# A decoder layer on one core: a new order of instructions, other buffers, and identity products in TensorE's planned waits

## The chip, the cores and the metric

The kernel runs on one core of a Trainium2 chip. The metric is the device time of one execution in microseconds. A core has five engines with their own instruction queues: TensorE (PE in the profile; its weight loads are shown as PEld), VectorE (DVE), ScalarE (ACT), GpSimd (POOL) and SyncE (SP), which here issues all transfers.

## The reference

One layer of a decoder, in float32, on `x` of 4 batches x 512 tokens x 512 features. Cut to what matters:

```python
x = x + attention(layernorm(x))        # gated delta rule, 16 heads, DK = 96, DV = 192
x = x + routed(layernorm(x), ctx)      # 64 sets a batch, the best 2 of 4 allowed ones
x = x + ffn(layernorm(x))              # 512 -> 2048 -> 512, ternary weights, 8-bit inputs

# attention: q, k, v = silu(causal conv of 4 taps (h @ W)); q and k normalized to length 1
# beta = 2 sigmoid(h @ Wb); g = -exp(A_log) softplus(h @ Wa + dt_bias); for each token, each head:
S = S * exp(g_t)
S = S + outer(k_t, (v_t - k_t @ S) * beta_t)
o_t = q_t @ S
# out = (o * rsqrt(mean(o * o) + eps) * norm_weight * silu(h @ Wg)) @ Wo
```

## The kernel before, in words

The recurrence is worked in chunks of 128 tokens (`NC` = 4 a batch). Inside a chunk it becomes a triangular system for each head, whose inverse is formed once. The work goes in 16 steps, one for each batch and group of four heads:

- `batch_head` (once a batch, stage "head"): loads `x`, normalizes it, transposes it on TensorE into `hT`, and computes the decays `egt`, `egs`, `egc` and `beta`.
- `keys`: `project4` projects four heads' keys. `project` is the common part: a weight tile `w`, four products of 128x512 into a PSUM bank `mm`, one ScalarE operation and three VectorE operations for the taps into `acc`. Then come transposes into `kt`, the decay matrix `dec` and the triangular matrix `lm`.
- `invert` (stage "inv"): 31 pairs of VectorE operations solve the 32x32 diagonal blocks, then products of 32x32 and 64x64 on TensorE join them.
- `queries`, and twice a step `pair` (two heads each): `values` (stage "value") projects and transposes the values through VectorE and through DRAM (`turn`), stage "gate" projects the gates, stage "rec" runs over the four chunks, stage "out" normalizes, gates, transposes through DRAM and multiplies by `Wo`.
- `ternary` (in three of the steps): makes the ternary weights. The 16 tiles of 128 tokens of `feed_forward` then run `route` (the sets) and `ffn`: products of fp8 weights, Silu, quantization, transposes in bf16, and the output product.

TensorE writes to eight PSUM banks: three `mm`, two `tp`, three `ch`. The rest lives in one SBUF tile `mem`, cut by the kernel into named slots (`acc` 6, `w` 6, `s` 16 and so on), which is why the profile calls all of them `mem`.

What sets the order: nothing of this is issued while the functions run. A `Recorder` notes each operation with its engine, a cost in us (`cost`), what it depends on and which slots it takes. `order` then plays a list scheduler: at each moment the engine that can start first takes, among its ready operations, the one that starts earliest and, among equals, the one with the earliest due time `due`. Due times are worked backwards from the ends of the steps, `PERIOD` apart; the work for the next step (`keys`, `invert`) is moved by `LEAD` steps, and the table `SHIFT` moves each stage and each pair of stage and engine. A slot is taken when an operation starts and is free again when its last user is done. `emit` issues the operations in this order, so each engine's queue is fixed before the kernel runs, and on the chip each engine works its queue in order and waits only for what an operation reads or overwrites. All instructions are issued in one line of `emit`, so the profile shows line 529 for nearly all; groups are told apart by the names of the PSUM banks and by shapes.

The constant `cst` holds the identity (`C_ID`) and three triangular masks; it is the fifth transfer in SP's queue, after the first four tiles of `x`.

Of the kernel before, what the change touches and what calls it, by code (L numbers as in the profile page):

```python
# [10 lines left out]
F32 = mybir.dt.float32  # L11
# [30 lines left out]
PERIOD = 122.1  # L42
LEAD = 0.95
PERIOD2 = 6.0
TERNARY = 7
SETUP = 12
WORDS = 53200
SHIFT = {
    "ffn": 7.2,
    "ffn gpsimd": -501.1,  # L50
    "ffn scalar": 226.0,
    "ffn tensor": -105.9,
    "ffn vector": -438.8,
    "gate": 13.2,
    "gate scalar": 366.7,
    "gate tensor": 48.8,
    "head": -306.9,
    "head gpsimd": 120.3,
    "head scalar": 380.7,
    "head tensor": 370.6,  # L60
    "head vector": 365.7,
    "inv": 43.1,
    "inv gpsimd": 87.6,
    "inv scalar": -17.2,
    "inv tensor": -19.3,
    "inv vector": -220.0,
    "keys": 66.8,
    "keys gpsimd": 154.5,
    "keys scalar": 1187.1,
    "keys tensor": -173.2,  # L70
    "keys vector": -244.9,
    "out": 73.2,
    "out gpsimd": 147.6,
    "out scalar": 80.4,
    "out tensor": 100.6,
    "out vector": -377.3,
    "query": 23.1,
    "query gpsimd": 248.2,
    "query scalar": -308.3,
    "query tensor": -17.1,  # L80
    "query vector": -276.0,
    "rec": -96.3,
    "rec scalar": 101.1,
    "rec tensor": -613.6,
    "rec vector": -466.5,
    "route": 23.3,
    "route gpsimd": 151.3,
    "route scalar": -481.0,
    "route tensor": -177.3,
    "route vector": 424.0,  # L90
    "tern": 18.9,
    "tern scalar": 117.0,
    "tern tensor": -135.8,
    "tern vector": 483.9,
    "value": -315.1,
    "value scalar": 255.5,
    "value tensor": -1022.2,
    "value vector": -580.5,
    "wo": 201.9,
    "wo scalar": -256.6,  # L100
# [205 lines left out]
class Recorder:  # L306
# [67 lines left out]
    def cost(self, op, engine, method, args, kw, outs, ins):  # L374

        n = max(free_elems(x) for x in outs[:1] + ins)
        if engine == "tensor":
            if method == "transpose":
                n = free_elems(args[2])
                return 0.12 if kind(args[1]) == F32 else 0.07  # L380
            m = free_elems(args[1])
            n = free_elems(args[2])
            if kind(args[1]) == F32:
                return max(n / 600.0, m / 555.0) + 0.012
            return max(n / 2400.0, 0.06 * m / 128) + 0.004
        if engine == "vector":
            if method == "scalar_tensor_tensor":
                return n / 960.0 + 0.21
            if method == "tensor_tensor_scan":
                return n / 480.0 + 0.21  # L390
            if method == "tensor_scalar" or (method == "tensor_copy" and not in_psum(ins[0])):
                return n / 1920.0 + 0.22
            return n / 960.0 + 0.15
        if engine == "scalar":
            f = args[2].name if method == "activation" else ""
            f = next((s for k, s in ACT_SETS.items() if f.lower() == k.lower()), None)
            op.table = f or op.table
            extra = (0.19 if "accum_out" in kw else 0.0) + (0.07 if len(ins) > 1 else 0.0)
            return n / 1230.0 + 0.2 + extra
        if engine == "gpsimd":  # L400
            if ALU.pow in args:
                return 0.155 * n + 0.44
            if method in ("tensor_tensor", "tensor_mul", "tensor_add", "tensor_sub"):
                return max(0.2, n * 0.0022 + 0.05)
            return n * 0.0009 + 0.235
        op.nbytes += outs[0].nbytes() if not isinstance(outs[0], View) else outs[0].ap.nbytes()
        return 0.38
# [13 lines left out]
    def order(self, period, shift):  # L421
# [23 lines left out]
        while len(done) < len(ops):  # L445
            best = None
            for e, queue in engines.items():
                pick = None
                for o in queue:
                    t = max(o.ready, clock[e])  # L450
                    if pick is not None and t > pick[0]:
                        continue
                    need = self.room(o)
                    if need is None:
                        continue
                    t = max(t, need)
                    if e == "scalar" and o.table not in (None, table):

                        key = (t, o.due + 2.6)
                    else:  # L460
                        key = (t, o.due)
                    if pick is None or key < pick[:2]:
                        pick = key + (o,)
                if pick is not None and (best is None or pick[0] < best[0]):
                    best = (pick[0], e, pick[2])
# [56 lines left out]
    def emit(self, tc, period, shift):  # L522
        self.done = self.order(period, shift)
        real = lambda x: x.real() if isinstance(x, View) else x
        with tc.manual_schedule():
            for o in self.done:
                engine = getattr(self.nc, o.engine)
                for method, args, kw in o.calls:
                    getattr(engine, method)(  # L529
                        *[real(x) for x in args], **{k: real(v) for k, v in kw.items()}  # L530
                    )
# [26 lines left out]
def decoder_layer(ctx: ExitStack, tc: tile.TileContext, a: dict, out: bass.AP):  # L558
# [23 lines left out]
    w.rec.emit(tc, PERIOD, SHIFT)  # L582
# [51 lines left out]
def attention(w, a):  # L634
# [15 lines left out]
    xs, wos, gs, tw, gw, vs, os_ = w.xs, w.wos, w.gs, w.tw, w.gw, w.vs, w.os  # L650
# [18 lines left out]
    t_wg = slots("wg", 1, [P, KC * GV])  # L669
# [15 lines left out]
    t_oq = slots("oq", 1, [P, HG * DV])  # L685
    t_o2 = slots("o2", 1, [P, DV])
    t_oT = slots("oT", 2, [P, GV])
    t_sq = slots("sq", 1, [P, NC * DK])
    t_b = slots("b", 12, [P, NC * H])
    t_s = slots("s", 16, [P, 4 * NC], ordered=False)  # L690
# [13 lines left out]
    def turn(src, blocks, there):  # L704

        dve.transpose(blocks, src)
        for q in range(P // BS):
            sp.dma_start(
                there[q], blocks[q * BS : (q + 1) * BS].rearrange("i (t j) -> i t j", j=BS)
            )  # L710

    def batch_head(b):
# [4 lines left out]
        for i in range(NC):  # L717
# [12 lines left out]
            act.copy(hT[:, :, i * P : (i + 1) * P], pt)  # L730
        pba = p_tp(P, NC, 2 * H)
        for t in range(NC):
            for kc in range(KC):
                pe.matmul(
                    pba[:, t], hT[:, kc, t * P : (t + 1) * P], wba[:, kc],
                    start=kc == 0, stop=kc == KC - 1,
                )
        sh = [P, NC, H]
        beta = s["beta"] = t_b(*sh)
# [4 lines left out]
        z = t_b(*sh)  # L744
# [21 lines left out]
        pgt = p_tp(H, NC, P)  # L766
        with rec.group():
            for t in range(NC):
                pe.transpose(pgt[:, t], g[:, t], ident)
        gT = t_acc(H, T)  # L770
        act.copy(gT, pgt.rearrange("h t p -> h (t p)"))
        sp.dma_start(gs[b], gT)
# [3 lines left out]
        pg = p_tp(P, 3, NC * H)  # L776
        pe.matmul(pg[:, 0], le, gf, start=True, stop=True)
# [7 lines left out]
    def project(wsrc, hT, taps):  # L785

# [12 lines left out]
        return acc  # L799

    def project4(key, f, hT, taps, t_dst):
# [3 lines left out]
        for i in range(3):  # L805
            rec.hold(*dst)
            acc = project(a[key][f, i], hT, taps[:, i])
            act.activation(dst[i], acc[:DK], AF.Silu)
            act.activation(dst[3][32 * i : 32 * i + 32], acc[DK:P], AF.Silu)
        return dst  # L810

    def keys(s, f):
# [4 lines left out]
        k = s["k"] = project4("wk", f, s["hT"], cqk[:, 0, f], t_k)  # L817
        kt = s["kt"] = [t_kt(P, NC, DK) for _ in range(4)]
        ss = t_s(P, 4, NC)
        for j in range(4):  # L820
# [6 lines left out]
            sq = t_sq(P, NC, DK)  # L827
# [103 lines left out]
    def queries(s, f):  # L931

        rec.stage = "query"
        q = s["q"] = project4("wq", f, s["hT"], cqk[:, 1, f], t_q)
        ssq = s["ssq"] = t_s(P, 4, NC)
        for j in range(4):
            pk = p_tp(P, NC, DK)
            sq = t_sq(P, NC, DK)
            rec.hold(sq)
            with rec.group():  # L940
                for c in range(NC):
                    pe.transpose(pk[:, c], q[j][:, c * P : (c + 1) * P], ident[:DK, :DK])
            act.activation(sq, pk, AF.Square)
            dve.tensor_reduce(ssq[:, j], sq, AX.X, ALU.add)
        pool.tensor_scalar(ssq, ssq, EPS * DK, EPS * EPS * DK, ALU.mult, ALU.add)
        for j in range(4):
            pa = p_tp(P, NC, P)
            with rec.group():
# [5 lines left out]
    def values(s, hg, jo):  # L954
# [3 lines left out]
        for vt in range(NVT):  # L958
            rec.hold(*vo)
            acc = project(a["wv"][hg, vt], s["hT"], cv[:, hg * NVT + vt])  # L960
            act.activation(acc, acc, AF.Silu)
            there = vs[s["b"], hg, :, vt * P : (vt + 1) * P]
            turn(acc, t_acc(P, T), there.rearrange("(t i) (c j) -> c i t j", i=BS, j=BS))
# [8 lines left out]
    def pair(s, hg, jo, last):  # L972

        h0 = hg * HG
        k, q, lm, mq, kt = s["k"], s["q"], s["lm"], s["dec"], s["kt"]
        egt, egc = s["egt"], s["egc"]
        vo = values(s, hg, jo)
        rec.stage = "gate"
# [3 lines left out]
        for c in range(NC):  # L982
            g = t_gate(P, HG, DV)
# [7 lines left out]
            act.activation(g.rearrange("p j v -> p (j v)"), pp, AF.Silu)  # L991
            gate.append(g)
# [6 lines left out]
        for c in range(NC):  # L999
# [3 lines left out]
            if c:  # L1003
# [4 lines left out]
                for j in range(HG):  # L1008
                    dve.scalar_tensor_tensor(
                        rz[:, j], pr[:, j], egt[:, c, h0 + j : h0 + j + 1], vo[c][:, j],  # L1010
# [22 lines left out]
            if c:  # L1033
# [4 lines left out]
                for j in range(HG):  # L1038
                    act.activation(oq[:, j], pq[:, j], AF.Copy, scale=egt[:, c, h0 + j : h0 + j + 1])
# [433 lines left out]
```

## Time and profile before

| | |
|---|---|
| median of 3 runs | 2455.29 us (2452.61 to 2458.24) |
| the profiled execution | 2456.92 us |
| its span, first to last instruction | 2455.1 us |
| mean granted TensorE clock | 0.961 |
| busy: DVE, ACT, POOL | 1928.6, 1291.9, 856.3 us |
| DMA | 294.66 MB, mean 120 GB/s |

PE is one of five engines that wait for each other; its busy time says how much of the span it worked, and the granted clock at what rate. A page's slice is a fortieth of the span, 61 us. The span holds three parts: a start in which the first inputs, keys and inverse are made (to about 170 us), the 16 steps, and from about 2100 us on the feed-forward tiles, the first of which run among the last steps.

### The profile page before, as it was taken

Reading aid. Unit: us, or ns where it says so; the run is one execution under the profiler, and the core shown is the slowest. Engines: PE = TensorE matmul, PEld = TensorE weight load, DVE = VectorE, ACT = ScalarE, POOL = GpSimd, SP = SyncE. Lnnn points to the kernel's source line nnn. Section 1 sums busy time; section 2 is a strip of 40 time slices with the busy share of each in tenths; the row PEclk is TensorE's granted clock in tenths of the full one; section 3 lists DMA queues with packets and bytes.
Section 4 is the critical chain, followed back from the end, with each engine's and each line's share of the span. In section 5 each row is a group of like instructions: output and inputs, shape, how many; then the busy total and the mean of one; then the engine's idle time right before and its main releaser. Section 6 shows DMA issues by size and latency. Waiting matters only on the chain.

```text
span 2455.1 us, 36566 instructions
## 1 busy us (share of the span) xinstructions
PE 2314.4 (94%) x12230; PEld 1412.0 (58%) x12230; DVE 1928.6 (79%) x3594; ACT 1291.9 (53%) x2780; POOL 856.3 (35%) x1275
## 2 busy tenths in 40 slices
PE   8869999999999999999999999999999999999886
PEld 5455656575565656575656565665656565644432
DVE  5888888887858788887978899886979786677653
ACT  4555554555454666564563645345466454645442
POOL 4042413334032333343232332333333331566653
PEclk9969999999999999999998999999999999999888
DMA  5446443635463555656655645663535444422000
GB/s 188 134 130 161 104 111 82 147 77 137 108 164 72 149 146 146 164 137 164 169 155 131 154 113 140 161 158 86 148 94 138 96 137 105 112 63 66 22 13 17
DMA packets 579003, 294.66 MB, mean 120 GB/s; under 512 B 424000, under 2 KB 495936, under 8 KB 578560
## 3 DMA queue, kind: packets, MB, share of 16 engines
q1 hardware_dynamic: 578816, 292.34, 45.8%
q8 instruction: 97, 1.59, 0.3%
q14 instruction: 90, 0.74, 0.1%
HBM read 223.93 MB, written 68.29 MB: 119 GB/s over the span
## 4 chain that ended last, share of the span: by engine, by line
PE 68%; DVE 18%; ACT 6%; POOL 5%; issue 3%; DMA 1%; SPq 0%; POOLq 0%; DVEq 0%; ACTq 0%
PE mm L529 42%; DVE mem L529 18%; PE ch L529 16%; PE tp L529 10%; POOL mem L529 5%; ACT mem L529 5%; ACT L529 1%; DMA vs<-mem 0%; DMA mem<-vs 0%; SPq L529 0%; DMA mem<-in_wv 0%; DMA mem<-in_x 0%; DMA tw<-mem 0%; POOLq L1469 0%; DVEq L529 0%
## 5 line engine op out<-in xcount | busy, mean ns | idle before, releaser
L529 PE MATMUL mm<-mem 128*128 128x512 f32 (+3 forms) x3760 | 1556.4, 551 | 33.7 <-issue 13.7
L529 POOL TENSOR_TENSOR mem<-mem 128x2 f32<-128x2 f32 (+4 forms) x864 | 713.0, 839 | 768.7 <-ACT mem L529 483.5
L529 PEld LDWEIGHTS mm<-mem 128*128 128x128 f32 (+2 forms) x3504 | 637.6, 193 | 559.8 <-issue 422.0
L529 ACT ACTIVATE mem<-mem 128x192 f32<-128x192 f32 (+5 forms) x1361 | 673.3, 523 | 511.4 <-DVE mem L529 323.3
L529 DVE SCALAR_TENSOR_TENSOR mem<-mm,mem 128x511 f32<-128x511 f32 (+4 forms) x656 | 465.1, 730 | 177.1 <-ACT mem L529 152.4
L529 PE MATMUL ch<-mem 128*128 128x192 f32 (+3 forms) x2688 | 559.5, 347 | 16.3 <-ACT mem L529 9.4
L529 PE MATMUL tp<-mem 32*32 32x32 f32 (+6 forms) x5782 | 395.5, 230 | 86.4 <-DVE mem L529 50.6
L529 PEld LDWEIGHTS ch<-mem 128*128 128x128 f32 (+2 forms) x2176 | 363.7, 186 | 138.7 <-issue 42.0
L529 PEld LDWEIGHTS tp<-mem 32*32 32x32 f32 (+3 forms) x5462 | 336.0, 141 | 183.4 <-issue 79.2
L529 DVE TENSOR_REDUCE mem<-mem 128x4 f32<-128x384 f32 (+29 forms) x660 | 332.4, 507 | 59.7 <-POOL mem L529 31.4
L529 POOL TENSOR_SCALAR mem<-mem 128x1 f32<-128x1 f32 (+2 forms) x352 | 123.0, 350 | 582.7 <-ACT mem L529 370.7
L529 DVE STREAM_TRANSPOSE mem<-mem 128x512 f32<-128x512 f32 (+3 forms) x368 | 279.3, 762 | 43.8 <-POOL mem L529 25.1
L529 ACT ACTIVATE mem<-mm,mem 128x512 f32<-128x512 f32 x192 | 130.8, 683 | 248.5 <-PE mm L529 248.1
L529 DVE TENSOR_TENSOR mem<-mem 128x64 f32<-128x64 f32 (+28 forms) x553 | 248.4, 450 | 15.4 <-POOL mem L529 2.2
L529 ACT COPY mem<-tp 32x512 f32<-32x512 f32 (+6 forms) x292 | 172.3, 602 | 84.3 <-PE tp L529 81.8
L529 PEld LDWEIGHTS <-mem 128*128 128x128 bf16 x1088 | 98.4, 104 | 156.5 <-issue 35.8
L529 DVE SCALAR_TENSOR_TENSOR mem<-ch,mem 128x192 f32<-128x192 f32 (+1 forms) x272 | 127.9, 507 | 66.2 <-PE ch L529 63.2
L529 DVE TENSOR_TENSOR mem<-mem,mm 128x512 f32<-128x512 f32 x144 | 97.7, 682 | 54.4 <-PE mm L529 52.9
L529 ACT ACT_TABLE_LOAD x87 | 111.6, 1283 | 28.9 <-DVE mem L529 26.9
L529 DVE TENSOR_TENSOR mem<-tp,mem 128x512 f32<-128x512 f32 (+1 forms) x132 | 86.8, 668 | 46.3 <-PE tp L529 35.8
L529 ACT COPY mem<-ch 128x384 f32<-128x384 f32 x128 | 60.8, 475 | 87.4 <-PE ch L529 86.5
L529 ACT ACTIVATE mem<-ch,mem 128x192 f32<-128x192 f32 x192 | 70.5, 416 | 53.9 <-PE ch L529 53.6
(27 smaller groups left out, 568.6 us busy)
## 6 DMA issues: line engine op xcount, KB each, us to landing
mem<-in_wg SPq DMA_DIRECT2D x32, 768.0 KB, 4.7
mem<-in_wv SPq DMA_DIRECT2D x96, 256.0 KB, 3.0
mem<-wos SPq DMA_DIRECT2D x96, 256.0 KB, 3.0
vs<-mem SPq DMA_DIRECT2D x384, 64.0 KB, 2.8
mem<-vs SPq DMA_DIRECT2D x128, 192.0 KB, 3.5
os<-mem SPq DMA_DIRECT2D x512, 48.0 KB, 2.7
mem<-os SPq DMA_DIRECT2D x128, 192.0 KB, 2.9
mem<-gs SPq DMA_DIRECT2D x64, 256.0 KB, 4.7
```

The source lines that it names most:

```text
L529: getattr(engine, method)(*[real(x) for x in args], **{k: real(v) for k, v in kw.items()})
```

## The change

- The constants of the order: `PERIOD` from 122.1 to 133.9, `LEAD` from 0.95 to 6.21, all of `SHIFT`; the index of an operation settles ties.
- The costs by which it plans: transposes and small products on TensorE, sums on ScalarE, element products on GpSimd.
- Buffers: `turn` of the values writes its blocks into the weight tile `w` that the projection has done with, no longer into a second `acc`; `s` has 14 slots in place of 16; the slots of `wg` and of the squares (`sq`, now `j`) may be taken in any order; some slots are claimed earlier or later (`hold`), and the product of keys and queries also needs `lm`.
- Products of the identity: `busywork` looks in the finished order for gaps of TensorE. A gap of t us gets (t - 0.8) / 0.219 products, rounded down, of the identity with itself (128x128, float32), into a PSUM bank that no one holds at that time by the order. `emit` issues them ahead of the operation that ends the gap. Nobody reads the result.

In the program built from it there are 373 such products in 42 runs. By their places in TensorE's queue: a run of 41 as its first instructions; runs of 81, 4, 6, 1, 3 and 9 around the first inversion and the first recurrence; 20 runs of 1 to 16 (87 products) in the middle; 15 runs of 1 to 33 (141) among the feed-forward tiles, the last four of 20, 20, 20 and 33. ScalarE's queue has 114 table loads in place of 87. Other kinds of instructions are as many as before, in other places of the queues.

```diff
-PERIOD = 122.1
-LEAD = 0.95
+PERIOD = 133.9
+LEAD = 6.21
 PERIOD2 = 6.0
+IDLE = 0.8
...
             if method == "transpose":
                 n = free_elems(args[2])
-                return 0.12 if kind(args[1]) == F32 else 0.07
+                return n / 600.0 + 0.008 if kind(args[1]) == F32 else 0.06
...
             if kind(args[1]) == F32:
-                return max(n / 600.0, m / 555.0) + 0.012
-            return max(n / 2400.0, 0.06 * m / 128) + 0.004
+                if m == BS:
+                    return 0.026
+                return max(n / 600.0, args[1].shape[0] / 600.0) + 0.006
+            return n / 2400.0 + 0.003
...
-    def emit(self, tc, period, shift):
+    def busywork(self, banks, weights, moving, most=99.0):
+        each = self.cost(None, "tensor", "matmul", (None, weights, moving), {}, [moving], [])
+        use = {}
+        for o in self.done:
+            for b in o.bufs:
+                if b.slots in banks:
+                    t = use.setdefault((b.slots, b.slot), {}).setdefault(b, [o.start, o.end])
+                    t[1] = max(t[1], o.end)
+        fill, at = {}, 0.0
+        for o in self.done:
+            if o.engine != "tensor":
+                continue
+            n = int((min(o.start - at, most) - IDLE) / each)
+            free = [k for k, u in use.items() if all(t[1] < at or o.start < t[0] for t in u.values())]
+            if n > 0 and free:
+                fill[o] = free[0][0].tiles[free[0][1]], n
+            at = o.start + o.cost
+        return fill
+
+    def emit(self, tc, period, shift, **busy):
         self.done = self.order(period, shift)
+        fill = self.busywork(**busy) if busy else {}
...
+                if o in fill:
+                    bank, n = fill[o]
+                    w, m = real(busy["weights"]), real(busy["moving"])
+                    for _ in range(n):
+                        engine.matmul(bank[:, : m.shape[1]], w, m, start=True, stop=True)
...
-    w.rec.emit(tc, PERIOD, SHIFT)
+    if IDLE:
+        banks = [s for s in w.rec.slots if s.name in ("mm", "tp", "ch")]
+        busy = {"banks": banks, "weights": w.cst[:, C_ID], "moving": w.cst[:, C_ID]}
+    w.rec.emit(tc, PERIOD, SHIFT, **(busy if IDLE else {}))
...
-    t_wg = slots("wg", 1, [P, KC * GV])
+    t_wg = slots("wg", 1, [P, KC * GV], ordered=False)
...
-    t_s = slots("s", 16, [P, 4 * NC], ordered=False)
+    t_s = slots("s", 14, [P, 4 * NC], ordered=False)
...
         for j in range(4):
             pa = p_tp(P, NC, P)
+            rec.need(s["lm"][:, j])
...
-            acc = project(a["wv"][hg, vt], s["hT"], cv[:, hg * NVT + vt])
+            acc, w = project(a["wv"][hg, vt], s["hT"], cv[:, hg * NVT + vt])
             act.activation(acc, acc, AF.Silu)
             there = vs[s["b"], hg, :, vt * P : (vt + 1) * P]
-            turn(acc, t_acc(P, T), there.rearrange("(t i) (c j) -> c i t j", i=BS, j=BS))
+            turn(acc, w.rearrange("p k c -> p (k c)"), there.rearrange("(t i) (c j) -> c i t j", i=BS, j=BS))
```

## The prediction

> **What bounds the kernel now.** I read the page first: busy time, PEclk row, chain.
>
> ```profile
> PE 2314.4 (94%) x12230; PEld 1412.0 (58%) x12230; DVE 1928.6 (79%) x3594; ACT 1291.9 (53%) x2780; POOL 856.3 (35%) x1275
> ...
> PEclk9969999999999999999998999999999999999888
> ...
> PE 68%; DVE 18%; ACT 6%; POOL 5%; issue 3%; DMA 1%; SPq 0%; POOLq 0%; DVEq 0%; ACTq 0%
> ```
>
> TensorE (PE) is busy 2314.4 of 2455.1 us and carries 68% of the chain that ended last. So three things can move the time: PE's work, the clock it runs at, and its idle time, 140.7 us. Second, the windows view, cut at the two places where the page changes character:
>
> ```profile
> 0.00:200.00 200.00, 160.51 (x826) 109.37 (x827) 154.83 (x303) 107.66 (x212) 67.82 (x94) 0.86 0.52 153
> 200.00:2100.00 1900.00, 1845.40 (x9936) 1148.54 (x9934) 1550.42 (x2851) 1015.58 (x2302) 586.54 (x848) 0.98 0.51 130
> 2100.00:2455.00 355.00, 308.53 (x1471) 154.06 (x1469) 223.38 (x441) 168.69 (x268) 201.95 (x333) 0.92 0.16 46
> ```
>
> The third number is PE's busy time, the third from the right the granted clock. The clock is low at the start (0.86) and in the feed-forward stage (0.92), and even the middle loses 2%. Third, the same view in steps of 3.4 us shows how it falls:
>
> ```profile
> 588.90:592.30 3.40, 1.60 (x22) 1.31 (x20) 2.77 (x5) 2.79 (x7) 1.57 (x3) 1.00 0.04 8
> 592.30:595.70 3.40, 3.40 (x4) 1.45 (x5) 3.33 (x6) 3.18 (x5) 0.83 (x1) 0.50 0.15 18
> ...
> 718.60:722.00 3.40, 3.40 (x39) 3.18 (x37) 3.40 (x6) 1.51 (x3) 0.00 (x0) 1.00 0.85 211
> 722.00:725.40 3.40, 3.40 (x18) 2.29 (x17) 3.13 (x4) 3.25 (x5) 0.00 (x0) 0.50 0.15 26
> ...
> 2404.80:2408.20 3.40, 1.07 (x16) 0.90 (x16) 0.00 (x0) 2.68 (x2) 0.00 (x0) 1.00 0.20 77
> 2408.20:2411.60 3.40, 3.01 (x8) 1.09 (x9) 0.00 (x0) 1.25 (x2) 0.00 (x0) 0.50 0.00 0
> ```
>
> A step in which PE was busy for 1.60 or 1.07 of 3.40 us is followed by one at clock 0.50. Stepping through the span, nearly all of the half-clock stretches follow a step in which PE was busy for less than about two thirds. The pair at 718.6 is another kind: PE was busy throughout, but with products of 64x64. The half-clock stretches add up to 192 us, and PE was busy in 157.8 of them: 36.7 before 200 us, 74 in the middle, 47.4 after 2100. Work at half rate takes twice as long, so full rate would have saved half of that: 18.4 + 37 + 23.7 = 79 us. At full clock PE's work is thus 2314.4 - 79 = 2235 us.
>
> Fourth, the waits of PE, longest first; all the groups give 134 us, the first 7.8 us among them:
>
> ```profile
> PE tp L529 <- DVE mem L529: 50.6, 18, 11.3
> PE tp L529 <- ACT mem L529: 35.0, 26, 8.1
> PE mm L529 <- issue: 13.7, 7, 4.5
> PE mm L529 <- DVE mem L529: 13.1, 15, 2.4
> ```
>
> In the timeline, 38 gaps of PE after its first product are over 0.8 us, together 95.5 us; by stage (to 200, to 2100, to the end) 28, 33 and 35.
>
> **The change, step by step.** The built program has the same instructions as before, in another order, but for 373 products of the identity on PE, in 42 runs, and 27 more table loads on ScalarE (114 for 87). Every other step of the edit (the tie in the scheduler's key, holds, fewer `s` slots) shows only through the order.
>
> *Price of a product.* A product is two passes of 128x128, float32. The nearest rows are the 96x128 ones; in the trace their passes follow each other every 112 ns at full clock and every 213 ns at half, so a product costs 0.224 or 0.426 us. In all: 373 x 0.224 = 83.6 us of PE. They cost nothing where PE would have waited, and this in full where it wouldn't.
>
> *The first run, 41 products.* It stands ahead of PE's first transpose and reads the identity out of the constant `cst`. These two rows of the timeline say when that can begin:
>
> ```profile
> 2.57 0.43 SPq L529 DMA_DIRECT2D mem<-in_cst  x1
> 7.82 4.37 PE L529 MATMUL tp<-mem 128*128 128x128 f32 x18 [7.82 <-DVE mem L529]
> ```
>
> `cst` takes 5.1 us to land, at 7.7, and the first input tile had been normalized at 5.9: PE's first wait ends with the constant, which the products need too. So they fill no wait but follow it. The clock of before rose at 12.0; until then 4.3 / 0.426 = 10 products, and 31 x 0.224 = 6.9 after it: the first transpose starts near 18.9 instead of 7.8. The transposes then run warm with all inputs ready, and the first projection starts at about 21.5 instead of 12.6: 9 us late. PE is nearly saturated from 7.8 to 51 us and what ends its waits after that (up to 11.3 us) is DVE's inversion, which starts from these products. Ends: 4 (part met by later waits) and 12 (clock a step later). I take **+9**.
>
> *The clock.* The other 332 products stand in 41 runs: 104 in the start (81 of them ahead of the first inversion, where before waits 11.3 us), 87 in the middle, 141 among the feed-forward products. A run leaves 0.8 us of its wait, so a step of 3.4 us that holds one wait of any length stays busy for three quarters, above what the rows show as the bound. In the feed-forward stage every drop follows a wait of 2.6 to 8 us, and the new order has a run of 5 to 33 there: I take 18 of 23.7. In the start, 41 us at half clock hold 32x32 and 64x64 products too, which keep their steps low: half, 9 of 18.4. In the middle I found about two thirds of the drops behind single waits over 0.8 us, the rest behind several short ones or small products; of the two thirds (25) a run meets perhaps two thirds: 16 of 37. Sum **-43**; ends -20 (the feed-forward stage and little else) and -62.
> The Trainium skill's page "TensorE: Matmul & The Clock Gate" (section "HAM oscillation — how this bites in real kernels") states that it takes an idle gap of over about 3.4 us to drop the clock, which speaks against products in short waits. The row at 588.9 shows a drop after 1.8 us of idle time in the step, so I follow the row; by the page only the drops behind waits over 3.4 us could be mended, some 24 us with all of them met, and the sum below would end near 2461.
>
> *The waits themselves.* A full clock makes PE reach its waits sooner, and the order is new. A run of n stands for a wait that the order holds of at least 0.8 + 0.224 n. The 41 runs: 41 x 0.8 + 332 x 0.224 = 107 us, against 95.5 seen before; by stage 28, 35 and 44 against 28, 33 and 35. So the order itself counts on more idle time at the end, where the last tiles wait for quantization on DVE, POOL and ACT. **+10**; ends -10 (other engines gain from the order too) and +35 (as many unforeseen ones again as foreseen).
>
> *Products that meet no wait.* PE executes them in order whatever the moment. The short runs hardly matter; I take a tenth of 332, 33 x 0.224: **+8**; ends 0 and +30.
>
> *Table loads.* 27 x 1.283 us = 34.6 us on ScalarE, 53% busy. PE's waits for ACT are 35.0 + 9.4 + 3.9 = 48 us against ACT's 1292 us of work, 4%: 1.4 us; the loads are nearer to urgent work than the mean, **+3**; ends 0 and +12. If ScalarE had no slack it would be 34.6.
>
> *Buffers.* The transposed values go into the weight tile `w` instead of a second `acc`. So an `acc` is free earlier, and a `w` is held some 8 us longer (taps, Silu, transpose, 2.8 us of DMA), with what follows on SP's queue, its next load, behind that. Six `w` tiles and 3.0 us per load hide it; PE's waits marked "issue" (13.7 us) are all that late loads can be now. In the queries, PE's product of keys and queries now also waits until DVE has made `lm`, and what is queued behind it on PE waits with it; the inversion, a step earlier, starts from the finished `lm`, so it is there. **0** for both; ends -6 and +6.
>
> Sum: 2455.1 + 9 - 43 + 10 + 8 + 3 = 2442.1 us of span. The profiled execution took 2456.92, 1.8 over its span, and the median of three runs is 2455.29, 1.6 below it: 2442.3, rounded **2442.5 us**.
>
> **Rivals.** *Products in the way* (slower). The order is fixed, and on the chip the waits shift by some us against it; a run whose wait is elsewhere delays the product behind it. Place: the long runs, 81 ahead of the first inversion and 14, 9, 16 and 13 in the middle. For: before's waits are short (2.4 us at most for mm on DVE), and the first run already misses. Against: the 11.3 us wait and those of the last tiles recur by structure. Without this term the sum gains 21 us; 21 / 0.224 = 94 of 332 products outside waits use that up. At half, 166 x 0.224 = 37 in place of 8: 2471.
>
> *The clock falls for another reason.* If small products and clusters of short waits decide outside the feed-forward stage, only about 20 us come back: 2455.1 + 9 - 20 + 10 + 8 + 3 = 2465. For: the row at 718.6, and the long half-clock stretch from 124.7 to 165.6, with full steps inside. Against: most steps before a drop are idle ones.
>
> *The order is the gain.* With the waits at their lower end, -10 in place of +10: 2422. For: the freer `acc`. Against: the order's own runs add up to more.
>
> **How the numbers follow.** Main case 0.52, its own range 2424 to 2461; products in the way 0.24; clock 0.14; order 0.10. No change means within 0.2%, 4.9 us, about what a measurement of this kernel can tell. Faster: 0.42 of the main case and the 0.10; the same: 0.11 from the upper edge of the main case and the lower edges of the two slow rivals; slower: the remaining 0.37. The range from 2415 to 2478 takes in most of all four.
>
> **What would show it.** PE's first transpose near 19 us; the products' passes at 112 ns; PEclk of 1 where the last tiles wait and a mean clock of about 0.98; PE busy near 2235 + 84 + 36 = 2355 us with under 100 us idle. Wrong if the clock stays at 0.96, if the products are followed by no wait, or if DVE or ACT end more waits than before.

## The result and the profile after

The changed kernel takes 2440.34 us (median of 4 runs, 2437.47 to 2443.09) against 2454.48 us for the kernel before in the same comparison: a ratio of 0.9938, 95% interval 0.9925 to 0.9950. The forecast was 2442.5. The sum came out, but the clock's share was put down to the products where much of it was the new order's, and two misses of some 5 us stood against each other; the experiments below show which.

The page of the changed kernel, its busy times, the granted clock by slice, and the chain that ended last:

```profile
PE 2354.8 (96%) x12976; PEld 1478.7 (61%) x12976; DVE 1940.5 (79%) x3594; ACT 1331.2 (55%) x2807; POOL 856.3 (35%) x1275
...
PEclk9989999999999999999999999999999999999999
...
PE 72%; DVE 15%; ACT 6%; POOL 3%; issue 2%; DMA 1%; SPq 0%; POOLq 0%; DVEq 0%; ACTq 0%
```

TensorE is busy 40 us longer than before, in a span of 2441.3 us that is 14 us shorter. The eights at the end of the clock's row, the feed-forward stage, have become nines. The windows view by stage says it in numbers (PE's busy time third, the clock third from the right):

```profile
0.00:200.00 200.00, 180.30 (x1080) 131.40 (x1081) 148.20 (x282) 109.70 (x208) 65.54 (x93) 0.94 0.49 146
200.00:2100.00 1900.00, 1857.70 (x10130) 1165.69 (x10129) 1561.51 (x2861) 1046.55 (x2310) 583.57 (x842) 0.99 0.51 131
2100.00:2441.00 341.00, 316.84 (x1768) 181.60 (x1766) 230.83 (x453) 174.96 (x292) 207.24 (x341) 1.00 0.17 48
```

The clock is 1.00 from 2100 us on, where it was 0.92. Half-clock stretches cover 61 us in place of 192, with 52 us of PE's work in place of 158: 20 in the start, 32 in the middle and none at the end, against 37, 74 and 47. The products make 88.6 of PE's 2354.8 us; its own instructions take 2266.2 us, 48.2 less than the 2314.4 of before.

The timeline of PE, first at the start, then around the wait before one of the last tiles' transposes (line 556 issues the products, line 558 everything else):

```profile
6.73 10.98 PE L556 MATMUL tp<-mem 128*128 128x128 f32 x82 [6.73 <-DMA mem<-in_cst]
17.55 1.04 PE L558 MATMUL tp<-mem 128*128 128x128 f32 x8
...
2409.36 4.63 PE L556 MATMUL tp<-mem 128*128 128x128 f32 x40
2414.68 1.07 PE L558 MATMUL tp<-mem 128*128 128x128 bf16 x16 [0.69 <-ACT mem L558]
2416.40 7.08 PE L558 MATMUL ch<-mem 128*128 128x512 fp8e4 x32 [0.66 <-ACT mem L558]
```

The first 82 passes (41 products) wait for the constant and hold the first transpose back until 17.55 us. At 2409 us, 20 products stand where PE waited, 0.69 us of idle time is left, and the 16 transposes behind it take 1.07 us; in the kernel before the same 16 took 1.89 us behind each of its last two waits.

### The profile page after: what moved, and what is told of

Its sections match the earlier page's. It is cut to its first block, busy times and chain, and to the rows that moved or that the text cites. A ratio compares the mean times of both kernels' runs of the same rounds, so it can differ in the third digit from the quotient of the medians.

```text
span 2441.3 us, 38049 instructions
## 1 busy us (share of the span) xinstructions
PE 2354.8 (96%) x12976; PEld 1478.7 (61%) x12976; DVE 1940.5 (79%) x3594; ACT 1331.2 (55%) x2807; POOL 856.3 (35%) x1275
## 4 chain that ended last, share of the span: by engine, by line
PE 72%; DVE 15%; ACT 6%; POOL 3%; issue 2%; DMA 1%; SPq 0%; POOLq 0%; DVEq 0%; ACTq 0%
PE mm L558 45%; PE ch L558 16%; DVE mem L558 15%; PE tp L558 10%; ACT mem L558 5%; POOL mem L558 3%; ACT L558 1%; PE tp L556 1%; DMA vs<-mem 0%; PE ch L556 0%; DMA mem<-vs 0%; SPq L558 0%; DMA mem<-in_wg 0%; DMA mem<-in_cst 0%; PE mm L556 0%
## 5 line engine op out<-in xcount | busy, mean ns | idle before, releaser
L558 PE MATMUL mm<-mem 128*128 128x512 f32 (+4 forms) x3760 | 1527.1, 543 | 20.1 <-issue 6.7
L558 PEld LDWEIGHTS mm<-mem 128*128 128x128 f32 (+1 forms) x3504 | 627.2, 190 | 536.5 <-issue 399.0
L558 POOL TENSOR_TENSOR mem<-mem 128x2 f32<-128x2 f32 (+5 forms) x864 | 714.3, 839 | 671.5 <-ACT mem L558 464.5
L558 ACT ACTIVATE mem<-mem 128x192 f32<-128x192 f32 (+6 forms) x1361 | 674.4, 524 | 454.9 <-DVE mem L558 307.0
L558 PE MATMUL ch<-mem 128*128 128x192 f32 (+3 forms) x2688 | 547.9, 342 | 30.8 <-DVE mem L558 18.9
L558 PE MATMUL tp<-mem 32*32 32x32 f32 (+7 forms) x5782 | 371.5, 225 | 23.9 <-ACT mem L558 15.0
L558 DVE TENSOR_REDUCE mem<-mem 128x4 f32<-128x384 f32 (+32 forms) x660 | 332.7, 506 | 64.2 <-POOL mem L558 33.5
L558 POOL TENSOR_SCALAR mem<-mem 128x1 f32<-128x1 f32 (+3 forms) x352 | 121.3, 345 | 576.3 <-ACT mem L558 378.5
L558 DVE STREAM_TRANSPOSE mem<-mem 128x384 f32<-128x384 f32 (+3 forms) x368 | 279.8, 763 | 50.9 <-ACT mem L558 24.0
L558 DVE TENSOR_TENSOR mem<-mem 128x64 f32<-128x64 f32 (+31 forms) x553 | 250.2, 454 | 16.5 <-POOL mem L558 1.9
L558 ACT ACTIVATE mem<-mm 128x384 f32<-128x384 f32 x128 | 61.9, 488 | 84.2 <-PE mm L558 83.5
```

What stands on the lines that cost most here:

```text
L558: getattr(engine, method)(*[real(x) for x in args], **{k: real(v) for k, v in kw.items()})
```

## The experiments

Ratios are to the kernel before on the same chip; 0.001 is 2.5 us. The experiments are told in three groups: the parts of the change, the products by place, and what the clock looks at.

### Parts of the change

**The new order and buffers without products.**

```diff
-IDLE = 0.8
+IDLE = 0.0
```

> The new order and buffers with no products at all (IDLE 0). Theory (the gain is the clock that the products keep): half-clock time with TensorE busy goes back from 52 us to some 150 us, a loss of about 50 us; 9 us of the start and some 10 us of products without a wait are saved: about 2470 us, mean clock near 0.96. Rival (the new order is the gain, the products cost what they take beyond waits): 2421 to 2440 us whatever the clock does.

Measured: 2451.29 us, ratio 0.9976 (0.9967 to 0.9985), so 6 us better than before, between the two theories. Its stages:

```profile
0.00:200.00 200.00, 162.98 (x843) 111.92 (x844) 153.58 (x298) 116.60 (x227) 68.21 (x99) 0.89 0.53 154
200.00:2100.00 1900.00, 1841.06 (x9974) 1144.85 (x9973) 1562.33 (x2872) 1048.07 (x2315) 589.46 (x853) 0.99 0.51 131
2100.00:2442.00 342.00, 289.41 (x1416) 146.69 (x1414) 221.22 (x426) 166.45 (x267) 199.04 (x324) 0.92 0.16 45
```

The clock of start and middle, 0.89 and 0.99, is already better than before's 0.86 and 0.98 with no product in the program; that of the end is not. PE's work at half clock is 22, 30 and 40 us by stage, against 37, 74 and 47 before. This profiled run is the fastest of its twelve, at a clock of 0.973 where the others have 0.967 to 0.971, so its 30 us in the middle are low: three more kernels below have this order and no products there (feed-forward runs alone, the wide margin, the constant first), and their traces show 45, 39 and 42 us. The order alone thus won about half of the work at half clock, and the products the end of the program and some of the rest.

**The old order with products**, by the same rule in the gaps of its own order, without a run ahead of the first transpose:

```diff
+            if n > 0 and free and at > 0.0:
+                fill[o] = free[0][0].tiles[free[0][1]], n
```

> The kernel before, its order and buffers unchanged, with products by the same rule in the gaps that its own order holds, without a run ahead of the first transpose: 230 products in 33 runs. Theory (products are the gain and the order little): mean clock from 0.961 to about 0.985, some 45 us of clock won, of which about 18 come back as waits and 4 as products without a wait: about 2432 us. Rival (the order is the gain): 2450 us or more.

Measured: 2442.71 us, ratio 0.9936 (0.9922 to 0.9950): products alone, on the order of before, are worth as much as the whole change with its first run, which these don't have. The clock rose to 0.974, less than I expected: 45 us of work at half clock stay in the start, 60 in the middle, 7 at the end.

**Buffers and tables apart.** The new buffers, holds and needs with the costs and tables of before, and the reverse:

> The new buffers, holds and needs, ordered with the costs, PERIOD, LEAD and SHIFT of before; no products. If the buffers are what makes the new order 6 us better without products: 2446 to 2452 us and fewer waits of TensorE. If it is the tables that fit them: no better than before, 2455 us or more, since the old tables were made for other buffers.

> The buffers of before, ordered with the new costs, ties, PERIOD, LEAD and SHIFT; no products. If the tables alone make the new order's 6 us: 2446 to 2452 us. If tables and buffers only work together: 2455 us or more.

```diff
-PERIOD = 133.9
-LEAD = 6.21
+PERIOD = 122.1
+LEAD = 0.95
...
-    "ffn": -286.8,
+    "ffn": 7.2,
```

(The edit of the first, cut: all of `SHIFT` and the body of `cost` go back too, and there are no products. The second makes the opposite edit in the kernel before. The new rule for ties is in both.) Measured: 2497.48 us, ratio 1.0153 (1.0135 to 1.0172), and 2501.66 us, 1.0177 (1.0161 to 1.0192). Neither half makes the 6 us; each alone costs some 40. The windows view of the second, from 2100 us on, shows one place: the last stage ends at 2499 us,

```profile
2100.00:2499.00 399.00, 344.63 (x1659) 182.93 (x1657) 258.15 (x493) 194.01 (x327) 211.82 (x357) 0.91 0.19 52
```

and PE's idle time between its first and last product is 167 us in the whole span, against 129 before. So the 6 us belong to tables and buffers as a pair; that tables fit only the buffers they were made for is the likely reason, but no run shows it. Which of the edits in them carries it stays open.

### The products by place

**Without the first 41.**

```diff
-            if n > 0 and free:
+            if n > 0 and free and at > 0.0:
```

> As the changed kernel, without the first 41 products (332 in 41 runs stay). Theory (they follow the constant's landing and delay everything behind): first transpose near 7 us in place of 17.6, and 9 to 10 us less in all, about 2431 us. Rival (later waits take the delay up): 2440 us. Third (they warm the clock for the start): gain of 4 us or less.

Measured: 2433.88 us, ratio 0.9903 (0.9887 to 0.9918), the best of all the kernels here. The first transpose starts at 7.82 us:

```profile
7.82 1.94 PE L558 MATMUL tp<-mem 128*128 128x128 f32 x8 [7.82 <-DVE mem L558]
```

Against the changed kernel that is 0.0035, 8.6 us by ratios and 6.5 by medians; the delay was 9.7 us at its place. So most of it stayed to the end.

**Feed-forward runs alone**, on the new order and on the old:

```diff
-            if n > 0 and free:
+            if n > 0 and free and o.step >= NB * NF4:
```

> The new order with products in the feed-forward runs alone (143 in 16 runs, one of 2 of them a little ahead). Theory as it stands now (nearly all that the products win is the feed-forward stage: without them TensorE worked 40 us at half clock there, 54 us elsewhere; with them 0 and 52): 2451 - 18 = 2433 us or a little less, since the long first run and the products that met no wait are gone. Rival (the prediction's split: 9 of the start and 16 of the middle are the products' too): 2451 - 18 = 2433 less nothing, against 2425 for all runs but the first, so 5 to 10 us over the kernel without the first run: 2439 to 2444 us.

> The order of before with products in the feed-forward runs alone (103 in 11 runs). If the feed-forward stage is what products win: as the old order with all its 230 products, 2443 us, within 3 us. If start and middle count: 2448 to 2452 us.

Measured: 2436.59 us, 0.9912 (0.9899 to 0.9926), and 2439.24 us, 0.9937 (0.9923 to 0.9950). From no products to these: 0.0064 on the new order and 0.0063 on the old, 15.5 us both times. From these to all but the first run: 0.0009 on the new order and 0.0001 on the old, 2 us and nothing, inside the intervals. (In the first expectation the figures of the rival were muddled, and the measurement lies between its number and the theory's. On the old order 0.9937 and 0.9936 speak for the theory.) So of 332 products, about 140 at the end carry the gain; the 190 before them pay for themselves at best.

They do not do so by leaving the clock alone. Start and middle with the feed-forward runs alone, and then with all but the first run:

```profile
0.00:200.00 200.00, 162.96 (x842) 111.87 (x843) 154.41 (x297) 116.08 (x226) 67.68 (x97) 0.89 0.53 153
200.00:2100.00 1900.00, 1840.51 (x9929) 1143.03 (x9929) 1555.07 (x2851) 1043.48 (x2299) 582.89 (x842) 0.99 0.51 131
...
0.00:200.00 200.00, 180.90 (x1033) 129.64 (x1034) 155.26 (x300) 116.84 (x227) 68.88 (x100) 0.97 0.53 155
200.00:2100.00 1900.00, 1855.97 (x10150) 1166.70 (x10149) 1559.63 (x2861) 1046.86 (x2308) 589.02 (x848) 0.99 0.51 131
```

Over all five runs of each the mean clock is 0.979 to 0.982 in the first and 0.988 to 0.992 in the second, and PE's own instructions take 2285.7 and 2266.9 us in the two traces. The 189 products win these 19 us and cost 189 x 0.224 = 42 us of PE, of which only a part fills idle time (121 us with the feed-forward runs alone, 88 us with all but the first run).

**Only products that a wait follows.** In the trace of the changed kernel, seven runs (3, 9, 2, 3, 4, 9 and 13) end with TensorE's next work 0.11 us after the last pass's start. They are taken out, with the first run:

```diff
+        order = list(fill)
+        for k in (0, 5, 6, 10, 13, 17, 18, 23):
+            del fill[order[k]]
```

> The changed kernel without the first 41 products and without the seven runs (43 products) that no wait followed, TensorE's next work starting 0.11 us after the last pass; 289 products in 34 runs stay. Theory (such products delay all behind them at their full price): 43 x 0.224 = 9.6 us less than without the first run alone, about 2424 us. Rival (TensorE's later waits take them up): 2434 us. Somewhere between if some lie ahead of waits on engines that keep their own time.

Measured: 2434.48 us, ratio 0.9904 (0.9887 to 0.9922): no difference from taking out the first run alone. In the two traces PE's busy time fell by 2.4 us only (2343.6 to 2341.2), while its work at half clock rose from 37 to 51 us, and its idle time rose from 88 to 92 us. How much of that comes from the edit and how much from run to run, one trace of each cannot tell; the time excludes the 9.6 us.

**The constant first.** The feed-forward runs alone, and `cst` as the first transfer:

```diff
-        self.done = self.order(period, shift)
+        self.done = sorted(self.order(period, shift), key=lambda o: o.index > 0)
```

> As the feed-forward runs alone, and the constant with the identity is issued as the first transfer instead of the fifth, all else in the same order. TensorE's first wait ends with the constant's landing at 7.4 to 7.8 us; issued 1.8 us earlier, the first tile of x becomes the last to wait for: first transpose near 6.3 us, 1 to 1.5 us less in all than with the feed-forward runs alone. If the start is bound elsewhere: no difference.

Measured: 2437.37 us, 0.9928 (0.9914 to 0.9941): no gain. The first transpose starts at 7.45 us against 7.00 in the profile with the constant fifth; the first tile of `x` is now read at 4.09 us instead of 3.45 and normalized at 7.40 instead of 5.91, and PE starts on that.

### What the clock looks at

**Narrow products and transposes** in the products' places, for the same time:

```diff
-                        engine.matmul(bank[:, : m.shape[1]], w, m, start=True, stop=True)
+                        engine.matmul(bank[:BS, : m.shape[1]], w[:, :BS], m, start=True, stop=True)
```

```diff
-                    for _ in range(n):
-                        engine.matmul(bank[:, : m.shape[1]], w, m, start=True, stop=True)
+                    for _ in range(2 * n):
+                        engine.transpose(bank[:, : m.shape[1]], m, w)
```

> The changed kernel with the same 373 products, as long as before (128 moving columns, two passes), but on 32 of the 128 weight columns. If the clock follows TensorE's busy time: as the changed kernel, 2440 us and clock 0.988. If it follows how much of the array works: clock back to about 0.965 and 2465 to 2475 us.

> The changed kernel with two transposes of the identity (one pass each) in the place of each product (two passes), so TensorE is as long at work. If transposes hold the clock like products: 2440 us and clock 0.988. If a transpose is not work to the clock gate: half-clock time as without products, clock 0.970, and the products' time on top of the 2451 us of that kernel where they meet no wait: 2451 to 2470 us.

Measured: 2441.62 us, 0.9933 (0.9914 to 0.9951), clock 0.989; and 2442.70 us, 0.9939 (0.9924 to 0.9955), clock 0.986. Both are the changed kernel over again, so neither a quarter of the columns nor a transpose costs time here by counting for less. In the last stage, where the changed kernel has none, the traces show 3.4 and 6.8 us of work at half clock, behind steps at 0.59 and twice at 0.56; a small difference is not excluded.

**A wider margin**, 1.6 us of each wait left idle, feed-forward runs alone:

> Products in the feed-forward runs alone, leaving 1.6 us of each wait in place of 0.8 (97 products in 10 runs). A step of 3.4 us with 1.6 to 1.8 us idle is busy for 0.47 to 0.53; in the traces so far steps at 0.54 and below let the clock fall and steps at 0.59 and above hold it. By that the clock falls again behind most of the last tiles' waits, some 30 us of work at half clock: 2445 to 2451 us. If it takes an idle gap of over 3.4 us, none is left: 2437 us, as with the margin of 0.8.

```diff
-IDLE = 0.8
+IDLE = 1.6
```

Measured: 2442.13 us, 0.9938 (0.9925 to 0.9952), some 6 us worse than with 0.8, and between the two expectations. In every trace here the half-clock stretches begin and end on a grid of 3.41 us; the windows view in these steps says why:

```profile
2335.80:2339.20 3.40, 1.56 (x20) 1.16 (x20) 2.17 (x8) 3.10 (x4) 2.23 (x9) 1.00 0.20 77
2339.20:2342.60 3.40, 3.20 (x9) 1.00 (x8) 0.00 (x0) 1.57 (x3) 0.17 (x1) 0.50 0.02 5
...
2410.90:2414.30 3.40, 1.81 (x22) 1.62 (x21) 0.00 (x0) 2.00 (x1) 0.75 (x1) 1.00 0.20 77
2414.30:2417.70 3.40, 2.74 (x21) 1.39 (x18) 0.30 (x1) 1.93 (x2) 0.00 (x0) 1.00 0.02 5
```

A step busy for 1.56 us (0.46) is followed by half clock, one busy for 1.81 us (0.53) is not. Cut on that grid, in this trace's last stage five steps at 0.43 to 0.49 let the clock fall, and four at 0.53 to 0.56 held it. The bound there lies at about half a step. It is no rule for other places: a step at 0.54 (2015.6 us in the kernel before) and one at 0.51 (1733.8 us in the changed one) were followed by half clock, in the last stage without products steps at 0.55, 0.57 and 0.58 (2307, 2327 and 2348 us) were and steps at 0.51 and 0.52 (2286 and 2406 us) were not, and in the kernel before a step at 0.43 (762.9 us) was not. What else counts, beside the busy time that the profile shows, stays open.

## Why the prediction was right, and where its steps were not

**The first run** (+9): right, 8.6 us by ratios. Its mechanism, that the products follow the constant's landing and fill no wait, is the first row of the timeline above; the first transpose starts at 17.55 us, forecast 18.9.

**The clock** (-43): right in size and put down to the wrong part. PE's own instructions take 48 us less. (By the rule that half of the work at half clock is lost, the fall from 158 to 52 us would be 53.) I gave the products all three shares, 18 for the feed-forward stage, 9 for the start, 16 for the middle, and the order nothing. The feed-forward share holds: without products PE works 40 us at half clock there, with them none, which is 20 us of work and 15.5 us of time on either order. Start and middle had 110 us at half clock in the kernel before. The new order without products there has 52, 67, 68 and 63 us in the traces of four kernels: no products, feed-forward runs alone, wide margin, constant first. With products there PE's own work at half clock is 46, 32, 46, 38 and 47 us: the changed kernel, then without the first run, only products that a wait follows, narrow products, transposes. Halved, the means of 62 and 42 us make some 24 us for the order and 10 for the products, where the forecast had 0 and 25. The step that failed is the guess that the products meet half of the loss in the start and two thirds of two thirds in the middle: the order of before with its own products keeps 60 of its 74 us in the middle, and 45 us in the start where it had 37.

**The waits** (+10): right in size. PE's idle time after is 86 us. The products' 84 us, less 11 for the first run and about 10 without a wait, stand for 63 more, together 149, against 141 before: 8 us more. Without products the new order's trace has 149 us as well.

**Products that meet no wait** (+8): right as a count of PE's time (43 products, 9.6 us, and not 33), wrong as a price. Taking them out gains nothing, as said above. The rival built on this term, products in the way, is refuted with it: its price per product of 0.224 us showed in the time only at the start.

**Table loads and buffers** (+3 and 0): not separated. All of the order with its loads and buffers, without products, is worth -6 us (0.9976), of which my sum had +3 for the loads, 0 for the buffers and most of the +10 for the waits, and no gain. But the pair is not a sum of parts: each half costs 40 us alone.

**The other rivals.** "The clock falls for another reason" is right in that products there bring back less than I took, and wrong about its price, since the order did there what the products did not. "The order is the gain" holds for 6 of 14 us.

So the total was met partly by luck. In the traces PE's own work fell by 48 us where the sum had 43, and products and idle time together, 88.6 us more of the one and 54.3 less of the other, rose by 34 where the sum had 30 (9 + 10 + 8 + 3); the two misses cancel. And the saving came only in part from what the forecast named, as the order stood in for the products in start and middle.

By ratios, from one kernel to the next, the change divides into order and buffers -6, feed-forward products -15.5, the others -2 and the first run +8.6. That these make the measured -15 (0.9938) is no check, since each is a step between the same ends.

## What to carry to other kernels

Keep TensorE busy where a stage makes it wait by structure, tile after tile, and look for these places in the windows view by steps of the clock; here 140 products at the end were worth 15.5 us, and 190 elsewhere raised the clock and cost as much as they won. A filler is free only if what it reads is there before the wait begins: the run of 41 waited for its constant and then held the first transpose back by 9.7 us. And the new tables with the old buffers, like the old tables with the new buffers, cost some 40 us, so buffers and order are to be changed and judged together.

## What the runs showed of the hardware

- The clock fell after steps of 3.4 us in which TensorE had been idle for little over half, most of them in single waits of 1.8 to 2.0 us (1.56 us busy of 3.40, then 0.50), though not after every such step. The Trainium skill's page "TensorE: Matmul & The Clock Gate", section "HAM oscillation — how this bites in real kernels", asks for an idle gap of over about 3.4 us; the measurement decides.
- Transposes hold the clock nearly as products do (0.986 against 0.988, where the runs without either have 0.967 to 0.973). The same page, section "Part 4: PE-mode transpose", says that a transpose does not count as busy in the same way; this trace doesn't agree.
- Exceptions stay open: steps filled with products of 64x64 (718.6 us in the kernel before, 225 us with the feed-forward runs alone) are followed by half clock although PE shows busy throughout; no run here isolates them, since the narrow products of 128 rows tried only fewer columns.
